# Two attention layers in fp32: the prologue's second weight sums, a fourth group of factors on VectorE, and the last block's scale

## The chip, the cores and the metric

The kernel runs on one core of a Trainium2 chip. The metric is device microseconds of one execution, the median of several runs. Before the change it is 2826.93 us in three runs (2825.17 to 2827.36). The core's engines are TensorE (PE, with its weight loads as PEld), VectorE (DVE), ScalarE (ACT), GpSimd (POOL) and SyncE (SP), which issues the transfers.

## The reference

Eight images x of 512 channels by 1024 positions go through two attention layers, all in fp32. Layer 0 has a group norm over 32 groups, one product for q, k and v, eight heads of 64 channels, and a projection; layer 1 has a group norm over 8 groups, one head of 512 channels, and a projection. Each adds its input to its output.

```
# layer 0
h = group_norm(x, 32)
q, k, v = per head: w_qkv @ h + b_qkv                 # 8 heads of 64
a = softmax_s(q.T @ k / sqrt(64)) applied to v
x = x + w_proj @ a + b_proj
# layer 1
h = group_norm(x, 8)
q, k, v = q_w @ h + q_b, k_w @ h + k_b, v_w @ h + v_b
out = softmax(q.T @ k / sqrt(512)) applied to v
x = x + p_w @ out + p_b
```

## The kernel before

**Products with seven instead of eight multiplications.** A product of 512 by 512 weights with an image is cut into 2 by 2 blocks and made from seven products of sums of blocks, nested a second time inside in some places. The sums on the weights' side are made once, in the prologue, and kept in DRAM: `prepare` loads a weight by four transfers (L284) and has VectorE make the first sums (L287, L288); `keep` stores the seven sums (L293, one transfer of 1,792 KB); `keep2` makes the second sums, those of the nested form, on GpSimd (four additions of L312) and stores them by seven transfers (L314, 448 KB each). `load_weight` (L325) fetches what is next in a list of uses into one of the weight buffers (L333), a 1,792 KB or a 1,344 KB half at a time. The sums on the image's side are made per image: `image_factors` gives a list t of closures for the first sums (L149 to L172), `inner_factors` (L408) a list ih for the nested ones (inner0 to inner6, four operations each on GpSimd by default, L419 and L434 being where they and their users stand in the trace).

**Folded weights.** Two products of weights are taken in the prologue: m from those of layer 1's queries and keys, z from those of its values and projection. `product` (L832) makes them, stores them to DRAM, and `prepare` reads them back. `bias_products` (L848) makes three vectors with 12 small products, writes them to a row on partition 0 (L858), stores them (L859) and loads them as columns (L862).

**The prologue** (`prologue`, L869 on) loads the weights and the first image, makes the sums of v, q and k, and computes v, q and k of image 0. Then it has, in the order of the text: the second sums of m on GpSimd; the transposed weights of v (`natural`), product z, the bias products; then the sums of p, p's stores, and the sums of z, which are hooked into the first attention.

**Layer 0's attention** (`attention0`, L637) runs over four pairs of heads (hp) and two halves of the positions (tb). A block (hp, tb) has eight score tiles sc on PE, each 128 by 1024, which ACT turns into e by an exponential (L656) and VectorE adds up (L658, L660); then av, 32 matmuls. Three PSUM buffers hold sc. After both halves of a pair, `reciprocals` (L591) adds over the partitions with a matmul of ones (the sums of the profile), stores the rows, loads them as 128 by 16 (cols, L620), takes reciprocals on VectorE (L622), stores them and loads them broadcast as r; `scale` (L688) multiplies a with r (L690 holds the operation) and, through `store`, sends a to kept in DRAM. The scaling of one pair runs inside the next pair.

**Hooks.** Each block calls two lists of `extra`: one after its scores, one after its av matmuls have been issued, so that 16 slots, numbered 0 to 15, carry other work in the order written: slot 9 and on the sums of the next image (`plan`, L1118), slots 1, 3, 5 and 7 of the first image the normalization of image 1 (L138 on ACT), and `later` the rest of the prologue. `keep_in_program_order` holds an instruction to its place on its engine; a scheduler places the others. All the kernel's transfers are issued by SP in one order, and an instruction that waits holds back those behind it.

**A round over images.** For image b the kernel runs layer 0's attention, then for b > 0 layer 1's scores of image b - 1 (`layer1_scores`, with the g convolution and `scores1`: L157 to L159 and L723 on VectorE), `layer1_rest` with layer 1's values (`values1`, L784), then `values` of the next image, and the projection. The hp 3 scale of attention has no next pair to run in: `attention0` returns it in `scaled` and `behind`.

Of the kernel before, what the change touches and what calls it, by code (L numbers as in the profile page):

```python
# [29 lines left out]
def two_attention_blocks_kernel(  # L30
# [8 lines left out]
    nc = tc.nc  # L39
    B, C, T = x.shape  # L40
    KC = C // P
# [132 lines left out]
    def main_path(ctx):  # L174
# [18 lines left out]
        def acc_tile(name):  # L193
            return ps_acc.tile([P, HT], F32, tag="acc", name=name)
# [30 lines left out]
        def finish():  # L225
            while tail:
                tail.pop(0)()
# [64 lines left out]
        def keep(n, t):  # L292
            nc.sync.dma_start(wdram[n], t)  # L293
# [4 lines left out]
        def keep2(n, t, engine=nc.gpsimd):  # L298

            if engine is nc.gpsimd:  # L300
                u = wpool.tile([P, 4, 7, P], F32, tag="w", name=f"prepare2_{n}")
                u = [u[:, i, :, :] for i in range(4)]
            else:
                u = [big_tile(f"prepare2_{n}_{i}", (P, 7, P)) for i in range(4)]
            quarter = lambda k, i: t[:, :, k, ts(i, P)]
            a11, a21, a12, a22 = quarter(0, 0), quarter(0, 1), quarter(1, 0), quarter(1, 1)
            s1, s2, s3, s4 = u
            for dst, x, y, op in (
                (s1, a21, a22, ALU.add), (s2, s1, a11, ALU.subtract), (s3, a11, a21, ALU.subtract),
                (s4, a12, s2, ALU.subtract),  # L310
            ):
                tc.keep_in_program_order(engine.tensor_tensor(dst, x, y, op))  # L312
            for j, f in enumerate((a11, a12, s4, a22, s1, s2, s3)):
                nc.sync.dma_start(wdram2[n][:, :, j, :], f)  # L314
# [7 lines left out]
        uses += [*twice["m"], "z"]  # L322
        loaded = []

        def load_weight():  # L325
            if uses:
                n = uses.pop(0)
                t = wpool.tile([P, 7 * C], F32, tag="w", name=f"w_{n[0]}_{len(uses)}")
                if isinstance(n, tuple):
                    t = t.rearrange("p (i j m) -> p i j m", i=4, j=7)  # L330
                    i = n[1]
                    t = t[:, : 4 - i]
                    nc.sync.dma_start(t, wdram2[n[0]][:, 4 * i : 4 + 3 * i])  # L333
                else:
                    t = t.rearrange("p (i k m) -> p i k m", i=7, k=2)
                    nc.sync.dma_start(t, wdram[n])
                loaded.append((n, t))

        def weight_part(n):
# [297 lines left out]
        def attention0(b, q, k, v, a, extra, store=None):  # L637
            n = 0
            scaled, totals, behind = [], [], []

            for hp in range(KC):
                for tb in (0, 1) if hp < KC - 1 or store else (1, 0):
                    uid = f"0_{b}_{hp}_{tb}"
                    total = pair_tile(f"sum_{uid}")
                    es = []
                    for s in range(NS):

                        sc = ps_pools[(0, 2, 1)[n % 3]].tile([P, 2, HT], F32, tag="sc", name=f"sc_{uid}_{s}")
                        n += 1
                        for j in range(2):  # L650
                            matmul(
                                sc[:, j, :], k[hp][ts(j, 64), ts(s, P)], q[hp][ts(j, 64), ts(tb, HT)],
                                start=True, stop=True,
                            )
                        e = pair_tile(f"e_{uid}_{s}")
                        nc.scalar.activation(e, sc, AF.Exp, scale=(C // 8) ** -0.5)  # L656
                        if s == 1:
                            nc.vector.tensor_add(total, es[0], e)  # L658
                        elif s > 1:
                            nc.vector.tensor_add(total, total, e)  # L660
                        es.append(e)
                    for f in extra.pop(0) if extra else ():
                        f()
                    av = acc_tile(f"av_{uid}")
                    for s in range(NS):
                        for j in range(2):
                            matmul(
                                av[ts(j, 64), :], v(s, 2 * hp + j),
                                es[s][:, j, :], start=(s == 0), stop=(s == NS - 1),
                            )  # L670
                    for f in [*scaled, *(extra.pop(0) if extra else ())]:
                        f()
                    dst = a[hp][:, ts(tb, HT)]
                    nc.scalar.copy(dst, av)  # L674

                    totals.append(total)
                    scaled = []
                    if hp < KC - 1 or store:
                        if tb == 0:
                            continue  # L680
                        dst = a[hp].rearrange("p (t n) -> p t n", t=2)
                    else:
                        dst = dst.rearrange("p (t n) -> p t n", t=1)
                    direct = store is None and (hp, tb) == (KC - 1, 0)
                    engine = nc.gpsimd if (b == 0 or hp == KC - 1) and not direct else nc.vector
                    scaled = []

                    def scale(hp=hp, dst=dst, totals=totals, uid=uid, direct=direct, engine=engine, scaled=scaled):  # L688
                        r = reciprocals(totals, uid, False, nc.scalar if direct else None)
                        scaled.append(lambda: tc.keep_in_program_order(engine.tensor_tensor(dst, dst, r, ALU.mult)))  # L690
                        if store:
                            scaled.append(lambda: store(hp))

                    totals = []
                    if store and hp == KC - 1:
                        behind.append(scale)
                    else:
                        scale()

            assert not extra  # L700
            return scaled, behind
# [103 lines left out]
        def raw(n, i):  # L805
            ts_ = [pair_tile(f"raw{n}_{h}") for h in range(2)]
            for kc in range(KC):
                nc.sync.dma_start(ts_[kc // 2][:, kc % 2, :], w[i, ts(kc, P), :])
            return [ts_[kc // 2][:, kc % 2, :] for kc in range(KC)]
# [55 lines left out]
        def prologue():  # L865
# [6 lines left out]
            wk = natural(raw_k, "k", ("a", "b"))  # L872
# [31 lines left out]
            t, steps = prepare("m")  # L904
            k = conv(weight_factors(first["k"][0]), hf, pcols("bk0"), "k0_0", hooks=[[], [], [], [], steps])
            finish()
            keep2("m", t)
            raw_p0 = raw("p0", 3)
            wv = natural(raw_v, "v", "bc")
            norm1.group_mean(acc_tile("gmean_0_1")[:, :KC])  # L910
            product(wv, raw_p, "z")
            norm1.affine(acc_tile("gvar_0_1")[:, :KC])
            bias = bias_products([(wk, "bq1"), (raw_p, "bv1"), (raw_p0, "bv0")])
            t, steps = prepare("p")
            for f in steps:
                f()
            keep("p", t)
            keep2("p", t)
            t, steps = prepare("z")
            later = {  # L920
                3: steps, 4: [lambda: keep("z", t)], 8: [load_weight], 10: [load_weight],
                12: [
                    load_weight,
                    lambda: tc.keep_in_program_order(nc.vector.tensor_copy(ubias, bias[0])),
                    lambda: tc.keep_in_program_order(nc.vector.tensor_add(obias[1], bias[1], pcols("bp1"))),
                    lambda: tc.keep_in_program_order(nc.vector.tensor_add(obias[0], bias[2], pcols("bp0"))),
# [166 lines left out]
        for b in range(B):  # L1093
# [20 lines left out]
            if last:  # L1114
                plan = {9: t[:2], 11: t[2:4], 13: [*t[4:6], *steps[:2]], 15: [*t[6:], *steps[2:4]]}
            else:
                plan = {
                    9: [*t[:2], lambda: ih[0](V)], 11: [*t[2:4], lambda: ih[1](V)], 13: [*t[4:6], lambda: ih[2](V)],  # L1118
                    15: t[6:],
                }  # L1120
            for i, fs in plan.items():
                extra[i] += fs
# [17 lines left out]

            kept = apool.tile([KC, P, T], F32, tag="kept", name=f"kept_{b}")
            scaled, behind = attention0(b, q, k, v, a, extra, lambda hp: nc.sync.dma_start(kept[hp], a[hp]))
            for f in ih[3:]:
                f()
            psum_pools(f"products_{b}", 2)
            tail.extend(behind)
            if b > 0:
                gf, gsteps = layer1_scores(b - 1, inner, [[], scaled])
                h, loads, applies = begun(load_x, norm0, b + 1, "h0")
                ahead, made = factors_ahead(h, loads, applies, f"h0_{b + 1}")  # L1150
                layer1_rest(b - 1, inner, gf, gsteps, [], [[]] * 4, ahead)
                v, norm0 = values(b + 1, made["inner"])
                inner = made["inner"]
            else:
                v, norm0 = values(1, inner, [[], scaled])

            again = [None] * KC

# [229 lines left out]
```

## Time and profile before

| | |
|---|---|
| median of three runs | 2826.93 us |
| the profiled execution | 2826.34 us |
| its span | 2824.6 us |
| granted TensorE clock, mean | 0.998 |
| busy: TensorE | 2788.6 us |
| busy: VectorE | 2020.2 us |
| busy: GpSimd | 1317.0 us |
| busy: ScalarE | 985.4 us |
| transferred | 320.10 MB, mean 113 GB/s |

The span runs from the first to the last recorded instruction; the execution takes 1.74 us more. Times in the views are counted from the span's start. The first image's attention and the second half of the prologue overlap between about 98 and 255 us; this is how the window answers show three stretches of it (columns: window, its length, busy us of PE, PEld, DVE, ACT and POOL with instruction counts, granted clock, busy share of the DMA engines, GB/s):

```profile
126.50:132.00 5.50, 5.50 (x28) 1.82 (x26) 5.29 (x3) 4.02 (x5) 5.42 (x3) 1.00 1.02 347
139.00:148.00 9.00, 9.00 (x44) 3.17 (x44) 8.47 (x7) 5.54 (x6) 0.00 (x0) 1.00 0.94 281
```

In the first the stores of p's sums have not begun and the transfers run at 347 GB/s; in the second the queue drains the second sums' stores, whose rows are short, at 281 GB/s with the DMA engines busy 0.94 of the time.

### The profile page before, as it was taken

To read this page: it belongs to the slowest core of one execution; us is meant where nothing else is said; L and a number is where in the kernel's file an instruction comes from. 1 tells how busy PE (TensorE), PEld (TensorE's weight loads), DVE (VectorE), ACT (ScalarE), POOL (GpSimd) and SP (SyncE) were. 2 spreads that over 40 slices of the span, in tenths; PEclk is the share of its full clock that TensorE was granted. 3 is DMA by queue.
4 is the path that set the end of the run, shared out by engine and by line. 5 is a ranking of instruction groups with operands and counts; after the bars stand their busy time and mean duration, and the time that the engine had idled before them with its cause. 6 is when DMAs were issued, how large, how long until landed. Compare 5 with 4: busy or idle time off the path is not lost.

```text
span 2824.6 us, 35089 instructions
## 1 busy us (share of the span) xinstructions
PE 2788.6 (99%) x12756; PEld 1749.0 (62%) x12756; DVE 2020.2 (72%) x2987; ACT 985.4 (35%) x1275; POOL 1317.0 (47%) x1331
## 2 busy tenths in 40 slices
PE   9989999999999999999999999999999999999999
PEld 5435735777367763768538685385844868338584
DVE  5568777677776777776777767767678766787665
ACT  1253363214542146321463125531255212633130
POOL 2404705736057450774417643275522946136672
PEclk9999999999999999999999999999999999999999
DMA  8643612245122441134411344014421135112302
GB/s 280 213 174 102 224 38 77 88 149 189 32 76 108 144 174 39 69 123 151 159 39 61 134 160 147 31 62 153 182 106 42 51 137 209 65 54 94 119 5 73
DMA packets 118526, 320.10 MB, mean 113 GB/s; under 512 B 19591, under 2 KB 57927, under 8 KB 107722
## 3 DMA queue, kind: packets, MB, share of 16 engines
q1 hardware_dynamic: 117758, 317.36, 31.6%
q8 instruction: 103, 1.69, 0.2%
q14 instruction: 77, 0.63, 0.1%
q10 hardware_dynamic: 588, 0.42, 0.0%
HBM read 247.13 MB, written 70.62 MB: 112 GB/s over the span
## 4 chain that ended last, share of the span: by engine, by line
PE 92%; DVE 4%; POOL 1%; issue 1%; DMA 0%; ACT 0%; DVEq 0%; POOLq 0%
PE sc L60 15%; PE av L60 14%; PE psb_av L60 6%; PE psb L60 5%; PE psa_av L60 4%; PE psc_av L60 4%; PE psc L60 3%; PE psa L60 3%; PE psb_z L60 3%; PE psb_k L60 3%; PE psb_q L60 3%; PE psb_v L60 3%; PE psb_g L60 2%; PE psb_p L60 2%; DVE sum L660 2%; PE psa_z L60 2%
## 5 line engine op out<-in xcount | busy, mean ns | idle before, releaser
L660 DVE TENSOR_TENSOR sum<-sum,e 128x1024 f32<-128x1024 f32 x384 | 489.5, 1275 | 35.5 <-ACT e L656 1.4
L656 ACT ACTIVATE e<-sc 128x1024 f32<-128x1024 f32 x512 | 476.2, 1048 | 87.5 <-PE sc L60 87.5
L60 PE MATMUL sc<-q,k 64*128 64x512 f32 x2048 | 458.5, 597 | 0.0
L60 PE MATMUL av<-e,v 128*64 128x512 f32 x2048 | 453.4, 595 | 0.0
L60 PEld LDWEIGHTS sc<-q,k 64*128 64x128 f32 x2048 | 191.0, 186 | 248.0 <-ACT e L656 119.0
L60 PEld LDWEIGHTS av<-e,v 128*64 128x64 f32 x2048 | 141.4, 137 | 299.0 <-issue 289.0
L419 POOL TENSOR_TENSOR inner_h<-t_h 128x256 f32<-128x256 f32 x76 | 62.8, 830 | 311.2 <-PE sums L60 262.7
L674 ACT COPY a<-av 128x512 f32<-128x512 f32 x64 | 37.6, 587 | 321.2 <-PE av L60 281.6
L126 POOL TENSOR_TENSOR rstd<-ve,mhalf 128x4 f32<-128x4 f32 x16 | 16.7, 1044 | 274.9 <-DVE ve L124 274.9
L658 DVE TENSOR_TENSOR sum<-e,e 128x1024 f32<-128x1024 f32 x64 | 82.8, 1293 | 86.7 <-ACT e L656 86.5
L60 PE MATMUL psb<-inner,inner_h 128*128 128x256 f32 x448 | 116.3, 382 | 5.4 <-POOL inner L434 5.3
L60 PE MATMUL psa_av<-e,z 128*128 128x512 f32 x256 | 113.3, 595 | 0.0
L690 POOL TENSOR_TENSOR a<-a,r 128x1024 f32<-128x1024 f32 (+1 forms) x11 | 27.4, 2490 | 155.7 <-DMA r<-all_rows 138.1
L60 PEld LDWEIGHTS psb<-inner,inner_h 128*128 128x128 f32 x448 | 83.9, 190 | 21.4 <-POOL inner L434 8.2
L737 POOL TENSOR_TENSOR sum<-sum,e 128x1024 f32<-128x1024 f32 x32 | 81.4, 2543 | 28.6 <-ACT e L733 27.4
L540 POOL TENSOR_TENSOR v<-v,v 128x256 f32<-128x256 f32 x28 | 20.1, 727 | 154.8 <-DVE u_v L535 154.8
L467 ACT COPY psb_v<-psa_v 128x512 f32<-128x512 f32 (+1 forms) x28 | 14.5, 517 | 221.1 <-DVE x L799 155.8
L723 DVE TENSOR_TENSOR e<-psc,u 128x512 f32<-128x512 f32 x56 | 38.6, 690 | 67.8 <-PE psc L60 67.8
L60 PE MATMUL psb_g<-inner_h,w_m 128*128 128x256 f32 x336 | 86.5, 385 | 0.4
L728 POOL TENSOR_TENSOR e<-e,e 128x512 f32<-128x512 f32 x64 | 80.5, 1273 | 11.5 <-DVE e L723 11.5
L60 PEld LDWEIGHTS psa_av<-e,z 128*128 128x128 f32 x256 | 48.0, 190 | 57.3 <-issue 56.6
L733 ACT ACTIVATE e<-e 128x1024 f32<-128x1024 f32 x64 | 65.1, 1052 | 45.7 <-DVE e L723 24.7
(433 smaller groups left out, 6095.5 us busy)
## 6 DMA issues: line engine op xcount, KB each, us to landing
r<-all_rows SPq DMA_DIRECT2D x78, 256.0 KB, 3.8
x<-in_x SPq DMA_DIRECT2D x36, 512.0 KB, 6.9
h<-in_x SPq DMA_DIRECT2D x32, 512.0 KB, 8.7
spill<-x SPq DMA_DIRECT2D x32, 512.0 KB, 4.0
x<-spill SPq DMA_DIRECT2D x32, 512.0 KB, 6.1
out<-x SPq DMA_DIRECT2D x64, 256.0 KB, 2.0
kept<-a SPq DMA_DIRECT2D x28, 512.0 KB, 2.6
again<-kept SPq DMA_DIRECT2D x28, 512.0 KB, 9.9
```

The costliest lines, as they stand in the source:

```text
L60: tc.keep_in_program_order(nc.tensor.matmul(*args, **kw))
L419: pin(engine.tensor_tensor(dst, x, y, ALU.subtract))
L540: nc.gpsimd.tensor_tensor(d, x, y, ALU.add)
L656: nc.scalar.activation(e, sc, AF.Exp, scale=(C // 8) ** -0.5)
L658: nc.vector.tensor_add(total, es[0], e)
L660: nc.vector.tensor_add(total, total, e)
L674: nc.scalar.copy(dst, av)
L690: scaled.append(lambda: tc.keep_in_program_order(engine.tensor_tensor(dst, dst, r, ALU.mult)))
L723: nc.vector.tensor_add(dst[0], ps, x[0])
L728: nc.gpsimd.tensor_tensor(blocks(dst, r, cc)[0], blocks(x, r, cc)[0], blocks(y, r, cc)[0], ALU.add)
L733: nc.scalar.activation(e[c, cc, r], e[c, cc, r], AF.Exp, scale=scale)
L737: on = lambda dst, x, y: lambda: tc.keep_in_program_order(nc.gpsimd.tensor_tensor(dst, x, y, ALU.add))
```

## The change

**Prologue.** p's four loads stand ahead of those of the third raw weight; p's first sums, its second sums on GpSimd (`keep2`) and both its stores stand ahead of product z, and the bias products too; z's first sums are hooked into slot 1 instead of 3, its store into slot 2 instead of 4, and the three weight loads of slots 8, 10 and 12 into slots 2, 2 and 5, now held to their place. **Scale.** In the first image, pairs 0 to 2 are scaled on VectorE, as in the other images. **Factors.** VectorE makes the fourth group of the list (inner6 by its name) in slot 11 too, so that GpSimd keeps three groups of seven; t[4] and t[5] go from slot 13 to slot 15. **Last block.** The scale of pair 3 and the store of it go from layer 1's g convolution to the start of the loads ahead in layer 1's values; in image 0 from the second to the fourth list of `values`' hooks. In the last block of the loop, what is scaled from pair 2 runs after the hooks of slot 15 instead of in slot 13.

```diff
--- before.py
+++ after.py
@@ -322,7 +322,7 @@
         uses += [*twice["m"], "z"]
         loaded = []
 
-        def load_weight():
+        def load_weight(pin=lambda ins: ins):
             if uses:
                 n = uses.pop(0)
                 t = wpool.tile([P, 7 * C], F32, tag="w", name=f"w_{n[0]}_{len(uses)}")
@@ -330,10 +330,10 @@
                     t = t.rearrange("p (i j m) -> p i j m", i=4, j=7)
                     i = n[1]
                     t = t[:, : 4 - i]
-                    nc.sync.dma_start(t, wdram2[n[0]][:, 4 * i : 4 + 3 * i])
+                    pin(nc.sync.dma_start(t, wdram2[n[0]][:, 4 * i : 4 + 3 * i]))
                 else:
                     t = t.rearrange("p (i k m) -> p i k m", i=7, k=2)
-                    nc.sync.dma_start(t, wdram[n])
+                    pin(nc.sync.dma_start(t, wdram[n]))
                 loaded.append((n, t))
 
         def weight_part(n):
@@ -668,13 +668,17 @@
                                 av[ts(j, 64), :], v(s, 2 * hp + j),
                                 es[s][:, j, :], start=(s == 0), stop=(s == NS - 1),
                             )
-                    for f in [*scaled, *(extra.pop(0) if extra else ())]:
+                    after = extra.pop(0) if extra else []
+                    if not (store and hp == KC - 1):
+                        after, scaled = [*scaled, *after], []
+                    elif tb == 1:
+                        after, scaled = [*after, *scaled], []
+                    for f in after:
                         f()
                     dst = a[hp][:, ts(tb, HT)]
                     nc.scalar.copy(dst, av)
 
                     totals.append(total)
-                    scaled = []
                     if hp < KC - 1 or store:
                         if tb == 0:
                             continue
@@ -682,7 +686,7 @@
                     else:
                         dst = dst.rearrange("p (t n) -> p t n", t=1)
                     direct = store is None and (hp, tb) == (KC - 1, 0)
-                    engine = nc.gpsimd if (b == 0 or hp == KC - 1) and not direct else nc.vector
+                    engine = nc.gpsimd if hp == KC - 1 and not direct else nc.vector
                     scaled = []
 
                     def scale(hp=hp, dst=dst, totals=totals, uid=uid, direct=direct, engine=engine, scaled=scaled):
@@ -904,23 +908,23 @@
             t, steps = prepare("m")
             k = conv(weight_factors(first["k"][0]), hf, pcols("bk0"), "k0_0", hooks=[[], [], [], [], steps])
             finish()
+            p0, p0_steps = prepare("p")
+            raw_p0 = raw("p0", 3)
             keep2("m", t)
-            raw_p0 = raw("p0", 3)
             wv = natural(raw_v, "v", "bc")
             norm1.group_mean(acc_tile("gmean_0_1")[:, :KC])
+            for f in p0_steps:
+                f()
+            keep2("p", p0)
+            keep("p", p0)
+            bias = bias_products([(wk, "bq1"), (raw_p, "bv1"), (raw_p0, "bv0")])
             product(wv, raw_p, "z")
             norm1.affine(acc_tile("gvar_0_1")[:, :KC])
-            bias = bias_products([(wk, "bq1"), (raw_p, "bv1"), (raw_p0, "bv0")])
-            t, steps = prepare("p")
-            for f in steps:
-                f()
-            keep("p", t)
-            keep2("p", t)
             t, steps = prepare("z")
+            load = lambda: load_weight(tc.keep_in_program_order)
             later = {
-                3: steps, 4: [lambda: keep("z", t)], 8: [load_weight], 10: [load_weight],
+                1: steps, 2: [lambda: keep("z", t), load, load], 5: [load],
                 12: [
-                    load_weight,
                     lambda: tc.keep_in_program_order(nc.vector.tensor_copy(ubias, bias[0])),
                     lambda: tc.keep_in_program_order(nc.vector.tensor_add(obias[1], bias[1], pcols("bp1"))),
                     lambda: tc.keep_in_program_order(nc.vector.tensor_add(obias[0], bias[2], pcols("bp0"))),
@@ -1115,8 +1119,8 @@
                 plan = {9: t[:2], 11: t[2:4], 13: [*t[4:6], *steps[:2]], 15: [*t[6:], *steps[2:4]]}
             else:
                 plan = {
-                    9: [*t[:2], lambda: ih[0](V)], 11: [*t[2:4], lambda: ih[1](V)], 13: [*t[4:6], lambda: ih[2](V)],
-                    15: t[6:],
+                    9: [*t[:2], lambda: ih[0](V)], 11: [*t[2:4], lambda: ih[1](V), lambda: ih[3](V)],
+                    13: [lambda: ih[2](V)], 15: t[4:],
                 }
             for i, fs in plan.items():
                 extra[i] += fs
@@ -1140,19 +1144,20 @@
 
             kept = apool.tile([KC, P, T], F32, tag="kept", name=f"kept_{b}")
             scaled, behind = attention0(b, q, k, v, a, extra, lambda hp: nc.sync.dma_start(kept[hp], a[hp]))
-            for f in ih[3:]:
+            for f in ih[4:]:
                 f()
             psum_pools(f"products_{b}", 2)
             tail.extend(behind)
             if b > 0:
-                gf, gsteps = layer1_scores(b - 1, inner, [[], scaled])
+                gf, gsteps = layer1_scores(b - 1, inner)
                 h, loads, applies = begun(load_x, norm0, b + 1, "h0")
                 ahead, made = factors_ahead(h, loads, applies, f"h0_{b + 1}")
+                ahead[0][:0] = scaled
                 layer1_rest(b - 1, inner, gf, gsteps, [], [[]] * 4, ahead)
                 v, norm0 = values(b + 1, made["inner"])
                 inner = made["inner"]
             else:
-                v, norm0 = values(1, inner, [[], scaled])
+                v, norm0 = values(1, inner, [[], [], [], scaled])
 
             again = [None] * KC
 
```

## The prediction

> **What bounds the kernel now.** I read the page's busy row first, then the matrix engine's waits, then the timeline around each wait. The busy row and the list of waits (line waited for: us in total, times, longest):
>
> ```profile
> PE 2788.6 (99%) x12756; PEld 1749.0 (62%) x12756; DVE 2020.2 (72%) x2987; ACT 985.4 (35%) x1275; POOL 1317.0 (47%) x1331
> ```
>
> ```profile
> PE sums L60 <- DVE sum L660: 12.4, 4, 8.6
> PE psb L60 <- POOL inner L434: 5.3, 6, 0.9
> PE tr_wk L63 <- DMA rawk<-in_w: 5.0, 1, 5.0
> PE psb_v L60 <- DVE u_v L535: 1.6, 1, 1.6
> ```
>
> TensorE works 2788.6 of 2824.6 us. The 36 us left are all there is to win, some 15 of them ahead of its first and behind its last matmul. The change neither adds nor removes a matmul, so it can act only through the short list above, or by making new waits. The timeline shows where the long ones lie and what holds the other engines there (start, us, work, count, [idle before <-releaser]):
>
> ```profile
> 118.21 1.39 SPq L211 DMA_DIRECT2D h<-in_x  x2
> ...
> 125.75 12.05 POOL L312 TENSOR_TENSOR prepare_p<-prepare_p 128x896 f32<-128x896 f32 x4 [6.34 <-DVE prepare_p L288]
> 126.86 14.68 DVE L660 TENSOR_TENSOR sum<-sum,e 128x1024 f32<-128x1024 f32 x6
> ...
> 129.22 1.30 ACT L138 ACTIVATE h<-h,b,s 128x1024 f32<-128x1024 f32 x1
> ...
> 143.18 4.65 SPq L284 DMA_DIRECT2D prepare_z<-product_z  x4
> ...
> 150.71 0.64 PE L60 MATMUL sums<-sum,ones 128*32 128x256 f32 x8 [1.16 <-DVE sum L660]
> ```
>
> ```profile
> 166.44 0.31 SPq L333 DMA_DIRECT2D w_k<-sums_k  x1
> 166.80 0.43 SPq L620 DMA_DIRECT2D cols<-rows  x1
> ```
>
> ```profile
> 174.92 0.25 DVE L622 RECIPROCAL recs<-cols 128x16 f32<-128x16 f32 x1 [13.72 <-DMA cols<-rows]
> ```
>
> ```profile
> 188.70 1.08 PE L60 MATMUL sums<-sum,ones 128*32 128x256 f32 x8 [8.62 <-DVE sum L660]
> 189.71 8.84 PE L60 MATMUL sc<-q,k 64*128 64x512 f32 x32
> ```
>
> See two things. While POOL sums prepare_p, VectorE's six sums take 14.68 us (2.45 each; the page's mean is 1.275), which makes PE wait 1.16. Then cols, queued behind a 1,792 KB load of w_k, lands 8 us after its issue; VectorE stands 13.72 us in the reciprocal behind it, its sums are late, and PE waits 8.62. PE is slow afterwards as well: the sums take 1.08 where the undisturbed ones take 0.64, and sc 8.84 where 7.07 is usual for 32. That is 0.44 + 1.77, about 2.2 more.
>
> **What the Trainium skill says.** "GPSIMD Engine Reference", Specifications: GpSimd shares its SBUF interfaces with VectorE and contends with VectorE instructions that have two SBUF inputs. The trace agrees: 2.45 against 1.28 us, and L312 itself takes 3.0 (12.05 / 4) here against 2.08 (8.32 / 4) at 98 us. "TensorE: Matmul & The Clock Gate", Part 1, says that an idle array falls back to a lower clock and needs some 3.4 us of work to recover; the slow sc after 8.62 us of idleness agrees, though the granted clock of the page does not show it. "DMA: Bandwidth & Descriptors", Queues, rings and completion order: each DMA engine takes a ring's descriptors in their order; here cols, behind w_k, landing at 174.9 agrees.
>
> **The change part by part.**
>
> *Projection's second sums (prologue).* The sums of p go from beside the first attention block to just after those of m, and their factors, loads and stores ahead of product z. Removed: 1.16 + 8.62 + 2.2, and 0.4 of ps_wz waiting for natv, which the bias matmuls, now put there, hide. Sum: 12.4. w_k leaves its place between rows and cols. The load on cols' path is now sums_z and two w_v: 1,792 + 1,792 + 1,344 KB, 4,928 KB, which is 5.05 MB, 13.7 us at the 368 GB/s of the window 151.5 to 166. Issued at about 150 they are through at 164 to 166; rows and cols then give cols at about 169, against 174.9. The six sums behind it end at about 188.6.
>
> What is added is on SP. Its order is now: loads of m, p and rawp0, seven stores of m, seven of p (448 KB each), the p sums' own store, bias_rows, product_z, bias_cols, prepare_z, and only then the four loads of h (image 1). Before, the first h went out at 118.21. I follow the chain:
> - POOL's sums of m take the buffer of prepare_k, so they wait for conv k's last matmul, about 100.3, and last 8.3: 108.6. VectorE's steps of p end beside them at about 110 to 111. POOL's sums of p take 8.3 more without the contention: 118.7 to 119.8.
> - The stores behind them took 10.3 us from the first issue to the last data before (137.83 to 148.1): 129 to 130 now.
> - The p store of 1,792 KB at about 330 GB/s is 5.5: 135. product_z (two of 512 KB) is 3: 137.5 to 138.
> - prepare_z waits for that landing and takes four issues (4.65 before, 3 at least), so h goes out at about 140.7. h took 3.5 to 5.9 us to land before: 144.2 to 146.6, I take 145.1.
>
> ACT's order has the first h apply (L138) behind the eight exps of the first block and ahead of the copy of a and all exps of the second. At 129.22 it cost nothing, h being there. Now ACT stands until 145.1; then h 1.3, copy 0.6, exp 1.05 give 148.05. PE has three sc buffers, and ends its third tile at 134.8 + 2.7 = 137.5. So PE waits 10.5 us. Its five remaining tiles then follow the exps at 1.05 instead of 0.89: 0.8. The clock restart costs what it did above, less what the exps' pace hides: about 1.2. Sum: 12.5 lost, 10 to 16 with the landing's and POOL's ends. Where the apply waits, the exps and the copy of a are queued behind it on ACT; PE waits for both, SP and VectorE follow.
>
> *First image's scale* (hp 0 to 2) moves from POOL (2.36 to 3.21 us each) to VectorE (1.22 to 1.29), between sums that do not end PE's wait by then: 0. Without that cover it would be 1.3 each.
>
> *Fourth group of factors.* VectorE makes inner6 too, four operations of 0.42, 1.65 us per image at slot 11; t4 and t5 and the scale of hp 2 go from slot 13 to 15. POOL has 12 factor operations instead of 16, needed over 10 us after. VectorE is through with the sums of block (3,1) at about 248 instead of 252.3, where PE wants them at 250.4, so the boundary wait of 1.98 goes, and 0.6 of the same kind in one later image (the fourth wait of the 12.4). But behind the first lies psb_v's 1.62 on u_v, which hangs on a chain over SP (kept of hp 2 after its scale, the load of ahead_1 behind it, its statistics, u_v). That chain starts at VectorE's scale at about 252 and ends u_v at about 263.1, 0.7 earlier than now. The boundary is worth 0.7 (between -0.5 and +2.5), the later image 0.6. For images whose boundary has no wait the moved operations cost nothing; their cover is ACT's exps.
>
> *Last block's scale.* In six images POOL's 2.35 us at 473.86, ahead of its factors, goes to layer 1's values, where POOL is idle from 549 to 560; its store now precedes the h loads by about 1.5 us, and those are needed 20 us later: 0. PE's wait on the factors, 0.88 x 6 = 5.3, goes. What is late next?
>
> ```profile
> 482.68 1.13 PE L60 MATMUL psb<-inner,inner_h 128*128 128x256 f32 x4 [0.88 <-POOL inner L434]
> ```
>
> ```profile
> 487.20 0.68 DVE L723 TENSOR_TENSOR e<-psb,c 128x512 f32<-128x512 f32 x1
> ```
>
> The matmul of psb that follows at 487.97 takes the bank that this addition has just read, and starts as it ends (487.88). VectorE's chain ahead of it (L533, L157, L159 from 481.9 without a gap) hangs on products of PE, not on POOL's factors. PE, early by 0.88, waits there instead: gain 0.05 per image (0 to 0.5), 0.3 in all. In values the multiply of psa (L797) now stands ahead of the two sz squares; sz is ready at about 562.5 where PE wants it at 563.14, so 0, or 0.5 per image lost if they contend.
>
> **Sum**: -12.4 + 12.5 - 0.7 - 0.6 - 0.3 = -1.5 us. From the profiled run's 2826.34 (span 2824.6 and 1.74 around it) this gives 2824.8; the median, 2826.93, lies 0.6 above that run, so 2825.2 is taken.
>
> **The rivals.**
> - *h lands early* (faster). If the ring mixes the stores so that product_z lands by 133, or POOL is done by 115, h lands by 140 and the stall is 5 to 7; if the psb wait goes entirely (5.3) and the boundary gives 2, the sum is about -12: 2814. For it: SP's issue of five p stores took only 5.3 us, so issue is ahead of data. Against: prepare_z must wait for product_z's data, and that is behind 1.8 MB of p on each engine's ring.
> - *The old wait comes back* (slower). Rows and cols of the first pair stand behind 5.05 MB instead of 3.1. My slack at sum (1,1) is 190.4 - 188.6 = 1.8 us; if cols lands later than about 171, each us beyond is a us for PE. At the old 8.62 with its restart, PE loses 10.8 on top of the new stall: 2836. For it: sums_z is issued only after VectorE's z steps, whose loads come last on SP. Against: the later PE is held, the later it wants the sums.
> - *Only traded.* If POOL takes 12.05 for p as now, h is 3 us later: 2828, within no change.
>
> **How the numbers follow.** Traded stall with the spread 10 to 16 and small gains: 0.50, reaching from 2820 to 2830. h early: 0.30, 2808 to 2820. The old wait back: 0.20, 2831 to 2840. Between these the range that leaves out 2 in 10 is 2814 to 2835; the likeliest case's own is 2820 to 2830. A measurement here tells 0.2%, 5.7 us, from no change. Faster than 2821.3: 0.30 and a little of the first case, 0.36; slower than 2832.6: 0.20 and a little, 0.22; within: 0.42.
>
> **What would show it.** Right: ACT's L138 idle from about 129 to 145 on DMA h; a PE wait of 8 to 13 us between 137 and 150 at sc, on ACT; no wait of sums at 150 and 188; L312 of prepare_p near 110 to 119; cols landing near 169; the six waits of psb on POOL replaced by six of about 0.8 on VectorE's L723; psb_v's wait on u_v still there. Wrong: h issued by 134, a wait of sums on VectorE at (1,1), or six gains of 0.88 with nothing behind them.

## The result, and the profile after

The changed kernel takes 2827.74 us (median of 14 runs, 2825.99 to 2829.55) against 2826.81 for the kernel before (14 runs beside them). The ratio is 1.0004, interval [0.9995, 1.0012]: no change that can be told. The forecast was 2825.2, no change the likeliest.

The profiled run of the changed kernel is its slowest, 2829.55, with a span of 2827.8. Some 1.1 us of its distance from before is a later first weight (5.0 us of waiting in one trace, 6.1 in the other, at code that did not change). The busy row and TensorE's waits of the changed kernel (line waited for: us in total, times, longest):

```profile
PE 2792.0 (99%) x12756; PEld 1755.4 (62%) x12756; DVE 2003.7 (71%) x3018; ACT 985.4 (35%) x1275; POOL 1273.1 (45%) x1300
```

```profile
PE sc L60 <- ACT e L656: 9.3, 1, 9.3
PE tr_wk L63 <- DMA rawk<-in_w: 6.1, 1, 6.1
PE psb_v L60 <- DVE v L535: 3.5, 1, 3.5
PE psb L60 <- DVE e L727: 3.2, 7, 0.5
PE psb_av L60 <- DVE u_av L240: 2.1, 5, 0.9
```

The total looks unchanged, but hardly a line of the list is the old one. The 12.4 of sums on VectorE and the 5.3 of psb on GpSimd are gone. New are a wait of sc on ACT (9.3), one of psb_v on an addition of VectorE (3.5), and short ones of psb and psb_av on VectorE.

Since TensorE runs the same matmuls in nearly the same order in both kernels, each matmul can be paired with itself. The difference of their starts, after less before, says where time went and came back:

| up to (start before, start after) | difference | step |
|---|---|---|
| first transpose (5.03, 6.13) | +1.10 | first weight's landing |
| first sc (120.73, 122.03) | +1.30 | +0.20, product z and its neighbours |
| sc of block (1,0) (151.27, 163.58) | +12.31 | +12.4 for the wait on ACT and the slow tiles after it, -1.4 for the sums of (0,1) |
| within sc of block (2,0) (191.58, 193.72) | +2.14 | -8.8 for the sums of (1,1), the rest for matmuls that are no longer slow |
| after the sums of (3,1) (253.04, 252.18) | -0.86 | -2.2, from +1.33 once the slow matmuls had ended |
| after the new psb_v wait (268.20, 271.74) | +3.54 | +4.4 |
| last matmul (2817.56, 2820.96) | +3.40 | -0.48 at psb in each of six images, +0.53 at psb_av in four of them and +1.2 in a fifth, -0.8 at the boundary of a later image, +0.3 at one psc_p |

The prologue's half, in the timeline of the changed kernel:

```profile
137.38 1.98 SPq L284 DMA_DIRECT2D prepare_z<-product_z  x4
139.40 1.92 SPq L211 DMA_DIRECT2D h<-in_x  x4
...
145.57 1.24 ACT L138 ACTIVATE h<-h,b,s 128x1024 f32<-128x1024 f32 x1 [14.87 <-issue]
146.72 0.56 ACT L679 COPY a<-av 128x512 f32<-128x512 f32 x1
147.19 2.85 ACT L656 ACTIVATE e<-sc 128x1024 f32<-128x1024 f32 x3
148.26 7.37 PE L60 MATMUL sc<-q,k 64*128 64x512 f32 x20 [9.30 <-ACT e L656]
...
164.44 0.61 SPq L617 DMA_DIRECT2D rows<-line  x1
166.24 0.32 SPq L620 DMA_DIRECT2D cols<-rows  x1
...
167.93 0.25 DVE L622 RECIPROCAL recs<-cols 128x16 f32<-128x16 f32 x1
...
191.75 1.07 PE L60 MATMUL sums<-sum,ones 128*32 128x256 f32 x16
```

The load of h is issued at 139.40, where before the first went out at 118.21. ACT stands 14.87 us in front of its first normalization, which needs that load (the view names no releaser, only "issue"). Behind that instruction, on ACT's one queue, are the copy of a and every exp of the second block, and so TensorE waits 9.30 us for an sc buffer. The sums of (1,1) then run 16 in a row with no wait: recs is made at 167.93 instead of 174.92. The queue has no part in that time. Rows goes out only at 164.44, after the sums of (0,1), which the stall has made late (162.58), and just before it the DMA engines are busy 0.02 of the time (columns as in the windows ahead of the prediction):

```profile
160.00:164.40 4.40, 4.40 (x34) 1.54 (x32) 0.68 (x1) 0.58 (x1) 0.00 (x0) 1.00 0.02 7
```

The boundary to values, first in the kernel before, then in the changed one:

```profile
235.18 0.33 SPq L1142 DMA_DIRECT2D kept<-a  x1
235.60 1.21 SPq L211 DMA_DIRECT2D ahead<-in_x  x2
...
258.50 1.95 PE L60 MATMUL psb_v<-w_v,inner_h 128*128 128x128 f32 x16
```

```profile
235.26 0.34 SPq L211 DMA_DIRECT2D ahead<-in_x  x1
...
251.76 1.75 DVE L694 TENSOR_TENSOR a<-a,r 128x1024 f32<-128x1024 f32 x1
253.53 0.33 SPq L1146 DMA_DIRECT2D kept<-a  x1
253.96 0.37 SPq L211 DMA_DIRECT2D ahead<-in_x  x1
...
259.39 1.29 DVE L91 BATCH_NORM_STATS2 bnst<-ahead 128x6 f32<-128x512 f32 x2 [3.98 <-DMA ahead<-in_x]
260.59 0.67 DVE L535 TENSOR_TENSOR v<-psb_v,c_v 128x512 f32<-128x512 f32 x1
261.32 3.78 PE L60 MATMUL psb_v<-w_v,inner_h 128*128 128x128 f32 x16 [3.51 <-DVE v L535]
```

Pair 2's scale, moved to slot 15, now runs at 251.76. The store of kept waits for it, and what stands behind that store on SP waits too. The first load of ahead is in front of the store and goes out at 235.26, about as before; the second, which went out at 236.09 before, goes out at 253.96. VectorE waits 3.98 us for its data in the statistics, with the addition that frees psb_v queued behind it. The sixteen matmuls that follow take 3.78 us where the same sixteen took 1.95 before.

### The profile page after: what moved, and what is told of

It is laid out like the page before. It is cut to its first block, busy times and chain, and to the rows that moved or that the text cites. A ratio compares the mean times of both kernels' runs of the same rounds, so it can differ in the third digit from the quotient of the medians.

```text
span 2827.8 us, 35078 instructions
## 1 busy us (share of the span) xinstructions
PE 2792.0 (99%) x12756; PEld 1755.4 (62%) x12756; DVE 2003.7 (71%) x3018; ACT 985.4 (35%) x1275; POOL 1273.1 (45%) x1300
## 5 line engine op out<-in xcount | busy, mean ns | idle before, releaser
L660 DVE TENSOR_TENSOR sum<-sum,e 128x1024 f32<-128x1024 f32 x384 | 470.5, 1225 | 35.6 <-ACT e L656 0.9
L419 POOL TENSOR_TENSOR inner_h<-x 128x256 f32<-128x256 f32 x16 | 14.8, 923 | 416.2 <-DVE x L1095 416.2
L126 POOL TENSOR_TENSOR rstd<-ve,mhalf 128x4 f32<-128x4 f32 x16 | 16.7, 1042 | 265.8 <-DVE ve L124 265.8
L419 POOL TENSOR_TENSOR inner_h<-h 128x256 f32<-128x256 f32 x30 | 26.7, 891 | 207.6 <-DVE h L1095 125.6
L727 DVE TENSOR_TENSOR e<-psc,u 128x512 f32<-128x512 f32 x56 | 38.6, 690 | 68.4 <-PE psc L60 68.4
L60 PE MATMUL psb_v<-w_v,inner_h 128*128 128x128 f32 x588 | 79.1, 282 | 3.9 <-DVE v L535 3.5
```

The lines of the kernel that those rows point to most:

```text
L60: tc.keep_in_program_order(nc.tensor.matmul(*args, **kw))
L126: nc.gpsimd.tensor_tensor(rstd, ve, mhalf, ALU.pow)
L419: pin(engine.tensor_tensor(dst, x, y, ALU.subtract))
L727: nc.vector.tensor_add(dst[0], ps, x[0])
```

## The experiments

All times are medians. Each kernel ran on one chip with the kernel before, whose median there was 2826.0 to 2826.5; the changed kernel's 2827.74 is from its own comparison. The diffs show only the lines that make the difference: where a transfer is held to its place, the argument that `load_weight` or `keep` gets for it is left out, and so are parts that an earlier diff shows.

### The first four: one cause each

**Normalizations later**, in the changed kernel:

```diff
-                plan = {2 * c + 1: [f] for c, f in enumerate(applies)}
+                plan = {s: [f] for s, f in zip((3, 5, 7, 8), applies)}
```

> The changed kernel with the four ACT normalizations of image 1 in slots 3, 5, 7 and 8 instead of 1, 3, 5 and 7, so that the late h is not waited for ahead of the second block. Theory (the late load of h is the whole price of the prologue's move): the 9.3 us wait of sc on ACT at 137 to 148 goes, with the slower tiles behind it (12.3 in all), and no sums wait comes back at (1,1): 2827.7 - 12.3 = 2815.5, 10 to 12 below before. Rival (the old wait comes back once PE is early: rows and cols stand behind sums_z and w_v): VectorE is late at the sums of (1,1), 3 to 9 us there, 2818 to 2825. Second rival (h lands so late that it holds another block): a wait of sc on ACT moves to about 165, 2820 or more.

Measured: 2823.25 us, ratio to before 0.9988 [0.9979, 0.9996], 4.5 below the changed kernel instead of the 12.3 expected. The wait on ACT is gone and the time falls in the first rival's range, but at another place than any of the three named: the sums of (0,1), not (1,1). The timeline of this kernel:

```profile
142.85 0.69 DVE L287 TENSOR_TENSOR prepare_z<-prepare_z 128x512 f32<-128x512 f32 x1 [8.64 <-DMA prepare_z<-product_z]
...
154.64 1.08 PE L60 MATMUL sums<-sum,ones 128*32 128x256 f32 x8 [4.03 <-DVE sum L660]
155.65 9.57 PE L60 MATMUL sc<-q,k 64*128 64x512 f32 x32
```

The first sums of z stand in slot 1, ahead of the sums of block (0,1) on VectorE, and wait for their own load until 142.85. In the changed kernel that was hidden, since ACT delivered no exps by then. With the exps on time, the sums of (0,1) are late, TensorE waits 4.03, and the 32 sc matmuls take 9.57 instead of 7.14. So the stall on h was all that the changed kernel lost here, but behind it stood another wait, some 7 us with its slow matmuls.

**Pair 2's scale back in slot 13**, in the changed kernel:

```diff
-                    if not (store and hp == KC - 1):
-                        after, scaled = [*scaled, *after], []
-                    elif tb == 1:
-                        after, scaled = [*after, *scaled], []
+                    after, scaled = [*scaled, *after], []
```

> The changed kernel with the scale of pair 2 back in slot 13, ahead of the next factors; t4, t5 and the fourth group stay where the change has them. Theory (the new wait of psb_v at 258 to 261 comes from SP: kept of pair 2 at 253.5 and, behind it, the load of ahead, for which VectorE stands 4 us): kept is issued near 239, the load before 250, the wait of 3.5 and the slow matmuls behind it go, and the sums of (3,1) still end in time: 2827.7 - 4.5 = 2823. Rival (the load is late for want of a buffer, whatever SP does): the wait stays, 2827.7 within 0.7.

Measured: 2823.54, 0.9990 [0.9982, 0.9999], 4.2 below the changed kernel, and the wait of 3.5 is no longer listed. In its timeline the store and the load behind it are back where they were:

```profile
234.89 0.33 SPq L1143 DMA_DIRECT2D kept<-a  x1
235.31 2.80 SPq L211 DMA_DIRECT2D ahead<-in_x  x2
```

The theory holds: SP's order, set by one VectorE instruction of 1.75 us, made the new wait. The older wait of psb_v on u_v (up to 1.8) is listed again, as in the kernel before.

**Last block's scale back in the g convolution:**

```diff
-                gf, gsteps = layer1_scores(b - 1, inner)
+                gf, gsteps = layer1_scores(b - 1, inner, [[], scaled])
-                ahead[0][:0] = scaled
-                v, norm0 = values(1, inner, [[], [], [], scaled])
+                v, norm0 = values(1, inner, [[], scaled])
```

> The changed kernel with the last block's scale back in layer 1's g convolution (for image 0 in the second list of values). Theory (that wait was only traded): psb waits 0.9 on POOL again in six images and PE waits no more at the next psb on VectorE, which costs 0.45 each; the waits of psb_av on u_av (about 0.5 in five images) go with it: net +2.7 - 2.6, 2827.7 within 1. Rival (the move is worth its whole 0.88 in each image): 2827.7 + 5.3 = 2833.

Measured: 2827.81, against 2827.74 for the changed kernel. Its waits:

```profile
PE psb L60 <- POOL inner L434: 5.3, 6, 0.9
PE psb L60 <- DVE e L727: 0.5, 1, 0.5
```

The 5.3 on GpSimd is back, six of the seven waits on VectorE's L727 and all of those of psb_av on u_av are gone, and the time is the same: traded, as the theory had it.

**Only w_k moved, in the kernel before**, from between rows and cols to behind the third pair's r:

```diff
                 12: [
-                    load_weight,
+                    lambda: load_weight(tc.keep_in_program_order),
```

> The kernel before with one transfer moved: the load of w_k from between rows and cols of the first pair to behind the third pair's r. Theory (the long wait of 8.6 is w_k ahead of cols on SP's queue, and the place of p's sums has little to do with it): cols lands near 169 instead of 174.9, recs is made near 169, the wait of sums at (1,1) falls from 8.6 to 3 or less: 2826.8 - 6 to - 11, 2816 to 2821. Rival (cols is late because the stores of p's second sums and w_v fill the queue; w_k adds nothing): the wait stays above 6, 2825 to 2827.

Measured: 2823.16, 0.9990 [0.9981, 0.9998]: 3.2 below before. Between the two expectations:

```profile
166.26 0.31 SPq L620 DMA_DIRECT2D cols<-rows  x1
167.92 0.25 DVE L622 RECIPROCAL recs<-cols 128x16 f32<-128x16 f32 x1 [9.61 <-DMA cols<-rows]
...
185.71 1.08 PE L60 MATMUL sums<-sum,ones 128*32 128x256 f32 x8 [4.87 <-DVE sum L660]
```

recs comes at 167.92, as the theory said, but the wait only falls from 8.62 to 4.87. Rows, issued at 155.88, still stands behind w_v and sums_z and lets cols go only at 166.26. The same 168 is early enough in the changed kernel, where TensorE comes 12 us later: its new stall covered what is left of the old wait.

### The next four: what stood behind, and on which engine

**Four moves together**: the normalizations and pair 2 as above, z's sums behind the sums of (0,1), and the large transfers behind the first pair's rows, cols and r.

```diff
-                1: steps, 2: [lambda: keep("z", t), load, load], 5: [load],
+                2: steps, 4: [lambda: keep("z", t, tc.keep_in_program_order), load, load], 6: [load],
```

> The changed kernel with four moves: the normalizations of image 1 in slots 3, 5, 7 and 8; z's first sums in slot 2, behind the sums of block (0,1), and z's store and the w_v and w_k loads in slots 4 and 6, behind the first pair's rows and cols; pair 2's scale in slot 13. Theory (h's landing, prepare_z's landing and the bytes ahead of rows are the three things that the prologue waits for, one behind the other): no sc wait on ACT at 137, no sums wait at (0,1) or (1,1), no psb_v wait of 3.5: 2827.7 - 12.3 - 4.4 = 2811, within 2. Rival (a further transfer takes their place, r or w_v for instance): one more wait of 3 us or over before 270, 2814 or more.

Measured: 2809.59 (five runs), 0.9941 [0.9928, 0.9955], 18.2 below the changed kernel, against 16.7 expected. Its waits have neither sc on ACT's exps nor sums on VectorE:

```profile
PE psb L60 <- DVE e L724: 3.2, 7, 0.5
PE psb_v L60 <- DVE u_v L535: 1.8, 1, 1.8
PE psb_av L60 <- DVE u_av L240: 0.9, 3, 0.3
```

**The same without moving the transfers** (and pair 2 as in the change): z's sums in slot 2, its store and w_v in slot 3.

```diff
-                1: steps, 2: [lambda: keep("z", t), load, load], 5: [load],
+                2: steps, 3: [lambda: keep("z", t), load, load], 5: [load],
```

> The changed kernel with the normalizations in slots 3, 5, 7 and 8 and z's first sums in slot 2, its store and w_v in slot 3: these are still ahead of rows and cols of the first pair, with 5 MB of transfers. Theory (the stall at sc hid an old wait: with PE 12 us earlier, cols comes too late for the sums of (1,1)): recs at about 166 to 168, a sums wait of 3 to 7 us near 180, 2818 to 2822. Rival (cols is in time, and the 4.0 of the first run was the last wait of the prologue): 2815.5.

Measured: 2821.38, 0.9985 [0.9979, 0.9992]. The timeline:

```profile
166.81 0.25 DVE L622 RECIPROCAL recs<-cols 128x16 f32<-128x16 f32 x1 [3.09 <-DMA cols<-rows]
173.90 1.23 DVE L694 TENSOR_TENSOR a<-a,r 128x1024 f32<-128x1024 f32 x1 [6.83 <-DMA r<-all_rows]
...
184.63 0.64 PE L60 MATMUL sums<-sum,ones 128*32 128x256 f32 x8 [4.51 <-DVE sum L660]
185.20 8.83 PE L60 MATMUL sc<-q,k 64*128 64x512 f32 x32
```

The old wait is back with 4.51 us, in the 3 to 7 expected. It comes by one step more than was expected: the sums of (1,0) were done by 163.7, ahead of recs, and what delays those of (1,1) is the first pair's scale, which now runs on VectorE ahead of them and waits 6.83 for r, two transfers behind recs. With all four moves recs is made at 154.3 and none of this shows.

**The fourth group back on GpSimd**, all else as changed:

```diff
-                    9: [*t[:2], lambda: ih[0](V)], 11: [*t[2:4], lambda: ih[1](V), lambda: ih[3](V)],
+                    9: [*t[:2], lambda: ih[0](V)], 11: [*t[2:4], lambda: ih[1](V)],
-            for f in ih[4:]:
+            for f in ih[3:]:
```

> The changed kernel with the fourth group of factors back on GpSimd, all else kept. Theory (the group is off PE's path on either engine): VectorE ends the sums of (3,1) 1.7 us or less earlier, which nobody waits for, and GpSimd ends its factors some 3 us later, about 263, which psb_v at that point doesn't need: 2827.7 within 1. Rival (the factors end too late on GpSimd): a wait of psb_v on POOL of 1 us or over in each of seven images, 2834 or more.

Measured: 2828.92, 1.0011 [1.0005, 1.0018], 1.2 above the changed kernel, with runs that overlap its own (2828.20 to 2830.77 against 2825.99 to 2829.55). No wait on GpSimd's factors appears, and GpSimd ends them at 258.7, not at the 263 expected. The theory is right on the path. In its trace psb_v waits 5.5 instead of 3.5 at the boundary, where VectorE stands 5.89 us for ahead and the order of the statistics differs; why the group's place alters that order was not followed up.

**The four moves, and the last block's scale traced behind the loads of h:**

```diff
-                ahead[0][:0] = scaled
+                ahead[0] += scaled
```

> The four moves of the run before last but two (the one with all of them late), and the last block's scale traced behind the loads of h in layer 1's values instead of ahead of them; this puts VectorE's multiply of psa behind the first sz addition again, as before the change. Theory (that order is what makes psb_av wait on u_av, about 0.5 in each of five or six images): these waits go, 2.5 us below the kernel with the four moves alone, about 2808.5. Rival (the waits come from GpSimd's scale or from later h loads): they stay, the same time within 0.7.

Measured: 2808.15, 0.9937 [0.9924, 0.9951], the fastest of all; 1.4 below the four moves alone instead of 2.5, with runs that overlap theirs (2807.26 to 2809.72 against 2808.01 to 2811.62). The waits of psb_av on u_av, of which the four moves had 0.9 left, are gone from the list. They depend on where this scale is traced; but in this trace VectorE's factor subtractions beside it also run in 1.28 us for two, where they took 2.34 in the changed kernel and with the four moves, so VectorE's order and the contention with GpSimd are not told apart.

### The last: was p's move needed?

**The kernel before, with only the order of transfers changed**: sums_z, w_v and w_k behind the first pair's r, p's second sums where they were.

```diff
-                3: steps, 4: [lambda: keep("z", t)], 8: [load_weight], 10: [load_weight],
-                12: [
-                    load_weight,
+                3: steps, 4: [lambda: keep("z", t, tc.keep_in_program_order), load, load], 6: [load],
+                12: [
```

(`load` is `load_weight` held to its place.)

> The kernel before, with p's second sums where they were, and only the order of transfers changed: the store of sums_z, the two w_v loads and the w_k load go behind the first pair's rows, cols and r. Theory (the long wait of the kernel before was all bytes ahead of rows and cols; the place of p's sums has part only in the 1.2 at (0,1)): recs near 160, no sums wait at (1,1), no slow matmuls behind it: 2826.4 - 10.8 = 2815.6, within 1.5. Rival (the stores of p's second sums at 129 to 144 delay the chain all the same, or VectorE is late from beside GpSimd): a sums wait of 3 us or over stays at (1,1), 2819 or more.

Measured: 2815.57 (five runs, 2815.23 to 2816.18), 0.9962 [0.9949, 0.9976], 10.9 below before. In its timeline:

```profile
151.45 0.64 PE L60 MATMUL sums<-sum,ones 128*32 128x256 f32 x8 [1.15 <-DVE sum L660]
...
159.11 0.25 DVE L622 RECIPROCAL recs<-cols 128x16 f32<-128x16 f32 x1 [2.23 <-DMA cols<-rows]
...
180.19 1.07 PE L60 MATMUL sums<-sum,ones 128*32 128x256 f32 x16
```

The wait of 8.62 and its slow matmuls are gone with p's sums in their old place, beside VectorE; the 1.15 that they cause at (0,1) stays. So the long wait came wholly from the bytes ahead of rows and cols.

## Why the prediction was right, point by point

**The trade in the prologue.** It named the new stall, its cause and its place, and the first run confirmed the cause. h was expected to go out at 140.7 and to land at 145.1; it went out at 139.40, and ACT began at 145.57. The loss was put at 12.5 and is 12.4, partly by luck. The wait, put at 10.5, was 9.5 by the pairing; the matmuls behind it, put at 2.0 (0.8 for the pace of the exps, 1.2 for the clock), lost 2.9. The exps set no pace there: it was ACT that waited for TensorE's tiles, 0.35 once and 0.68 twice. Of the gains, 1.2 and 10.8 were forecast at the two sums, and the table shows 1.4 and 11.0. The 0.4 of natv did not come off, since 0.6 of a new wait of sc on the last copy of product z and other small shifts stand against it (+0.2 in all up to the first sc).

That cols would land near 169 came true for another reason than the one given. The prediction derived it from 5.05 MB of transfers ahead of rows; in the trace these were through, and rows went out late because the stall held the sums. Also, the 10.3 us taken for p's second stores is that of the last five of seven: in the kernel before, two went out at 128.60 and 130.21, and the store of p's first sums at 125.64, so the window 126.5 to 132 shown ahead of the prediction already holds stores of p.

**The old wait as a rival.** The prediction priced it on top of the new stall, at a slack of 1.8 us. It did not come back on top, but it was there: the run with the stall and z's wait taken away met it at 4.5 us. The argument against it, that a later TensorE wants the sums later, is what the runs show. The Trainium skill, "DMA: Bandwidth & Descriptors", Queues, rings and completion order, bears on it as cited: rows and cols took their turn behind 5 MB, so that recs came 15.4 us after the copy of the sums (151.45 to 166.81, z alone moved); with these transfers behind them it was 4.1 (155.06 to 159.11, the last run).

**The boundary: the step that failed.** "The boundary is worth 0.7 (between -0.5 and +2.5)". The sums' wait went as forecast (2.2 by the pairing), but the chain that the prediction names there, kept of pair 2, the load of ahead behind it, its statistics, was moved the wrong way. It was taken to start at about 252 in both kernels and to end 0.7 earlier. In fact the kernel before had that store out at 235.18 and the load at 236.09; slot 15 put them at 253.53 and 253.96. The cost is 4.4, so that the boundary loses 2.2. The prediction named the transfers queued behind the moved instruction, but did not date them in both kernels.

**Last block.** "Gain 0.05 per image (0 to 0.5)" came to 0.48: VectorE's two sg additions took 1.82 instead of 2.30, which the estimate, holding VectorE's chain fixed, left out. GpSimd's factors ran some 2 us earlier against them; that this shortened them was not tested. Its loss in values, "0, or 0.5 per image lost if they contend", came to 0.53 in four images and 1.2 in a fifth. The sum, near nothing, is right by two errors of opposite sign (-2.9 and +3.3). The waits shown are 0.5, not the 0.8 named.

**First image's scale and fourth group.** Costed at nothing on the path. With the group on GpSimd the kernel is no faster, so no cost of having it on VectorE shows. The scale's place on VectorE shows no wait in the changed kernel, but in the run with z alone moved it holds the sums of (1,1) behind r: its cover, that VectorE is early, was the stall's.

**The sum.** -1.5 was forecast, +0.9 came by the medians. By the pairing of the two profiled runs it is +2.3 without the later first weight; the two figures cannot be brought closer, since the runs of each kernel spread over some 3 us and the changed kernel's profiled one is its slowest. The term that is most off is the boundary, by 2.9: +2.2 instead of -0.7. The rest of the sum holds within about 1.

## What to carry to other kernels

When a wait of many microseconds on one engine goes, look for the next one behind it in the same stage before counting the gain: here three stood in a row (h for ACT, the load of z for VectorE, rows and cols behind 5 MB on SP), and taking out one gave a third of its length. A small load on which a whole engine waits belongs ahead of the large ones on its queue; that order alone gave 10.9 us without moving any sums. And when an instruction is moved, date in both kernels every store and load that stands behind it, because a 1.75 us multiply put a load 18 us later.

## What the runs showed of the hardware

TensorE was slow for a while after the longer waits, and not in proportion to them. After 4.03 us idle the eight sums took 1.08 instead of 0.64 and the 32 sc matmuls 9.57 instead of 7.14, 2.9 in all. After 4.51 us the eight sums took 0.64, as undisturbed, and the 32 sc matmuls 8.83, 1.7 more.

The reason can be seen, though not on the page, whose clock row has slices of 70 us: the window views give the granted TensorE clock of any stretch (third figure from the end). First the kernel before, around its wait of 8.62, then the run with z alone moved, around its wait of 4.51:

```profile
180.00:182.90 2.90, 0.08 (x4) 0.00 (x0) 2.59 (x4) 0.15 (x1) 1.04 (x1) 1.00 0.10 24
183.00:193.10 10.10, 4.40 (x16) 1.72 (x18) 6.13 (x4) 1.02 (x1) 1.91 (x1) 0.50 0.13 53
193.30:196.00 2.70, 2.70 (x16) 1.27 (x14) 1.43 (x3) 2.48 (x3) 0.00 (x0) 1.00 0.03 2
```

```profile
182.50:185.40 2.90, 0.77 (x10) 0.36 (x12) 2.03 (x3) 0.00 (x0) 0.00 (x0) 1.00 0.07 25
185.45:188.80 3.35, 3.35 (x10) 1.33 (x10) 0.58 (x1) 1.02 (x1) 0.00 (x0) 0.50 0.01 3
188.90:192.00 3.10, 3.10 (x16) 1.34 (x16) 2.02 (x3) 3.08 (x4) 0.00 (x0) 1.00 0.01 1
```

TensorE ran at half clock, in a stretch that begins and ends sharply. By the clock records of the eleven traces, all such stretches except the one at the very end last 3.41, 6.83 or 10.24 us: 10.24 in the kernel before (182.95 to 193.19) and behind the stall of the changed kernel (143.72 to 153.96), 6.83 in the first run after 4.03 us idle, 3.41 in the run with z alone moved after 4.51. What is lost is half of TensorE's work inside the stretch. In the kernel before TensorE worked from 188.70 to 193.19 of it, 4.49 us, and lost 2.2; in the run with z alone moved it worked through all 3.41 and lost 1.7.

So the length of a wait does not fix its price. The 4.03 us wait was followed by twice the stretch of the 4.51 us one. Of the waits of about 2 us at the boundary to values, those of 1.98 (kernel before) and 1.85 (pair 2 back in slot 13) were followed by no stretch at half clock, those of 1.83 (four moves) and 1.99 (last run) by one of 3.41. The new wait of psb_v brought 6.83 in the changed kernel after 3.51 us, and 3.41 in the first run after 3.6. "TensorE: Matmul & The Clock Gate" of the Trainium skill (Part 1) has a free-running window of about 3.4 us in which the activity of TensorE is judged; lengths of one, two and three times 3.41 agree with it. What inside a window decides is not shown by these runs.
